# A graph kernel's prologue: the first block's rows gathered from x, row buffers placed lowest, fewer list loads

## The chip, the core and the metric

The kernel runs on one core of a Trainium2 chip. A core has five engines with their own instruction queues: TensorE (PE, with weight loads shown as PEld), VectorE (DVE), ScalarE (ACT), GpSimd (POOL) and SyncE (SP), which here only issues DMAs. All work in SBUF (128 partitions); TensorE writes PSUM. Times are microseconds of device time for one execution, and the metric is the median over executions. In the profile L12 means line 12 of the kernel, and `a<-b` means that an instruction writes tile `a` from tile `b`.

## What is computed

Two graph layers over the same 200,000 edges (`src`, `dst`, sorted by `dst`) and 6,250 nodes of 128 features. Cut to what matters here:

```python
h = jnp.maximum(_layernorm(x), 0.0)
# layer 0: attention over the edges that end in a node, 8 heads of 16
z = (h @ W).reshape(N, 8, 16)
el, er = einsum("nhp,hp->nh", z, attn_l), einsum("nhp,hp->nh", z, attn_r)
e = leaky_relu(el[src] + er[dst], 0.2)
a = exp(e - segment_max(e, dst)[dst])
x = x + segment_sum(z[src] * a, dst) / segment_sum(a, dst) + bias
h = jnp.maximum(_layernorm(x), 0.0)
# layer 1: a tensor product per edge, with weights from a small network on edge_attr_8
s, v = h[:, :32] @ W_up_s, einsum("nui,uw->nwi", h[:, 32:], W_up_v)
w = silu(silu(edge_attr_8 @ A1 + b1) @ A2 + b2) @ A3
x = x + segment_sum(products(s[src], v[src], edge_attr_4, w), dst) @ W_out
```

`z[src]` and `s[src], v[src]` are the costly part for data movement: each of the 200,000 edges takes one row of a table of nodes.

## The kernel before

Edges come in tiles of 128 (`P`), one edge to a partition, 1,563 of them (`TU`), and 16 tiles (`KB`) make a block, 98 blocks (`NB`) in each layer. Because the edges are sorted and the degrees even, the edges of a block end in few nodes, and a sum over edges is a matmul with a one-hot matrix. If the sorted ends are too uneven for that, a general kernel runs instead: a flag `ok_i` is computed first, all engines read it (`values_load`, L959) and branch (`tc.If`). Everything of the even case after the flag is in `even_edges`.

The prologue, in `tile_even_edges`, makes the table of layer 0. All of x (50 tiles of 128 nodes, in the order of a partition each, in chunks of 2, 3, 5, then 6 tiles, the last of 4) is loaded to `xs`. A loop over chunks runs as a software pipeline: mean and variance (`moments`), deviation, the normalised tile `fh` (shared out over ScalarE, VectorE and GpSimd by the tile's number), then groups of three tiles: transpose, relu to `h_t`, matmul with the extended weights `w_ext` (128 columns of z, 8 of el, 8 of er), copy to `zt`. z and el of a chunk go to the table `t0` in HBM (`to_table`, L792 to L798), er goes to `er_all` and is split into three bf16 parts in `er3`. Then GpSimd gathers the 16 row tiles of block 0 from `t0` into `z_first` (`gather`, L834: one indirect DMA for each tile of 128 edges, with the node numbers of `src_col`). The test for uneven edges compares each edge's end (`d_i`) with the one before it (`q_i`), two loads of the same list with a shift of one.

In `even_edges` SP first loads constants, then lists of ends, from which VectorE builds masks (`eq`, then `masks` on ScalarE), and the local ends `dloc`. A small transpose (`p_c`) gives `at`, the node numbers that SP uses to fetch single rows.

In the main loop the row tiles of a block lie in a buffer `g` of the pool `fz`, which has five (`z_pool`). GpSimd gathers them, up to three blocks ahead in the program; a buffer comes free when the sums of its block are done, a block later. In one block of three SP fetches the last tile by single rows (`rows_by_row`, L1078 to L1082, tile `r`), and in some blocks TensorE takes one tile out of a copy of the table in SBUF (`t0s`), which is loaded in the first four blocks (`split`, L1167).

Order. The order of TensorE, VectorE and ScalarE, in the main loops SP's too, is the order written (`tc.manual_schedule`). GpSimd and, in the prologue and the setup, SP are put in order by the framework from its own estimate. Each engine works its queue in order: what stands behind a waiting instruction waits too. Pools are laid out in SBUF in the order in which they are entered, and a tile that lies where an earlier pool's tile lay waits until that one's last reader and writer are done.

The pools at the head of `even_edges` are entered in this order:

```python
const = ctx.enter_context(tc.tile_pool(name="fconst", bufs=1))
z_pool = ctx.enter_context(tc.tile_pool(name="fz", bufs=5))
```

So the constants lie lowest, where the prologue's `fx` pool (`xs`, lists, weights) was.

Of the kernel before, what the change touches and what calls it, by code (L numbers as in the profile page):

```python
# [9 lines left out]
F32 = mybir.dt.float32  # L10
BF = mybir.dt.bfloat16
# [7 lines left out]
P = 128  # L19
# [722 lines left out]
def tile_even_edges(  # L742
# [46 lines left out]
    def to_table(table, of, i, n, eng):  # L789

        if i == 0:
            eng.dma_start(table[: P - W0, :], of[W0:, 0, :])  # L792
            if n > 1:
                to = table[P - W0 : n * P - W0]
                eng.dma_start(to.rearrange("(j p) f -> p j f", p=P), of[:, 1:n, :])
            return
        to = table[i * P - W0 : (i + n) * P - W0]
        eng.dma_start(to.rearrange("(j p) f -> p j f", p=P), of[:, :n, :])  # L798
# [20 lines left out]
    def deviation(pool, mv, n, name, m=P):  # L819
        rs = pool.tile([P, n, 1], F32, name=f"rs{name}")  # L820
        nc.scalar.activation(rs[:m], mv[:m, :, 1:2], AF.Sqrt, bias=eps[:m])
        return rs

    def normal(pool, mv, rs, n, name, m=P):

        nc.vector.reciprocal(rs[:m], rs[:m])
        mr = pool.tile([P, n, 1], F32, name=f"mr{name}")
        nc.vector.scalar_tensor_tensor(mr[:m], mv[:m, :, 0:1], -1.0, rs[:m], op0=OP.mult, op1=OP.mult)
        return rs, mr

    def gather(to, table, tiles, width, first=0):
        for t in tiles:
            k = first + t - tiles[0]
            nc.gpsimd.indirect_dma_start(  # L834
                out=to[:, k, :width], out_offset=None, in_=table,
                in_offset=bass.IndirectOffsetOnAxis(ap=src_col[:, t : t + 1], axis=0))
        return to

    def tiles_of(a, first):
        return a[first : first + TG * P * P].rearrange("(g t e) -> t g e", t=P, e=P)  # L840


    with tc.manual_schedule(engines={mybir.EngineType.PE, mybir.EngineType.DVE,
                                     mybir.EngineType.Activation}), \
# [11 lines left out]
        nc.scalar.sqrt(root, eps)  # L856
        w_ext = fx.tile([P, CW], F32, name="fw_ext")
# [9 lines left out]
        nc.sync.dma_start(src_col, srcc)  # L867
        d_i = fx.tile([P, TG, P], I32, name="fd_i")
        nc.sync.dma_start(d_i, tiles_of(dstt, P))
        q_i = fx.tile([P, TG, P], I32, name="fq_i")  # L870
        nc.sync.dma_start(q_i, tiles_of(dstt, P - 1))
        off = fx.tile([P, TG], F32, name="foff")
        nc.sync.dma_start(off, nums[:, NB * KB : NB * KB + TG])
# [7 lines left out]
        er_all = fx.tile([P, NX, H], F32, name="fer_all")  # L881
        NC = len(gx)
        mvs, rss, mrs, hs = {}, {}, {}, {}
        todo, done, outs = [], [], []
        for k in range(NC + 3):
            if 0 <= k - 1 < NC:
                rss[k - 1] = deviation(fp, mvs[k - 1], gx[k - 1][1], f"x{gx[k - 1][0]}")
            c = k - 2
            if 0 <= c < NC:
                i, n = gx[c]  # L890
                rs, mr = rss[c], mrs[c] = normal(fp, mvs[c], rss[c], n, f"x{i}")
                h = hs[c] = fp.tile([P, 10, P], F32, name="fh")
                for j in range(n):
                    by = (i + j) % 7
                    if by in ((2, 6) if c < NC - 2 else (2,)):
                        nc.scalar.activation(h[:, j, :], xs[c][:, j, :], AF.Identity,
                                             bias=mr[:, j, :], scale=rs[:, j, :])
                    else:
                        eng = nc.gpsimd if by in (0, 3, 5) and c < NC - 2 else nc.vector
                        eng.tensor_scalar(h[:, j, :], xs[c][:, j, :], mvs[c][:, j, 0:1],  # L900
                                          rs[:, j, :], op0=OP.subtract, op1=OP.mult)
            if k >= 3:
                i, n = gx[k - 3]
                zt = fp.tile([P, 10, CW], F32, name="zt")
                todo += [(k - 3, zt, j0, min(3, n - j0)) for j0 in range(0, n, 3)]
            while todo:
                c, zt, j0, m = todo.pop(0)
                p_t = fp_ps.tile([P, 4, P], F32, name="p_t")
                for j in range(m):
                    nc.tensor.transpose(p_t[:, j, :], hs[c][:, j0 + j, :], ident)  # L910
                h_t = fp.tile([P, 3, P], F32, name="h_t")
                nc.scalar.activation(h_t[:, :m], p_t[:, :m], AF.Relu)
                done.append((c, zt, j0, m, h_t))
                while len(done) > (1 if k < NC + 2 or todo else 0):
                    c, zt, j0, m, h_t = done.pop(0)
                    p_z = fp_ps.tile([P, 3, CW], F32, name="p_z")
                    for j in range(m):
                        nc.tensor.matmul(p_z[:, j, :], h_t[:, j, :], w_ext, start=True, stop=True)
                    outs.append((c, zt, j0, m, p_z))
                    while len(outs) > (1 if k < NC + 2 or todo or done else 0):  # L920
                        c, zt, j0, m, p_z = outs.pop(0)
                        copy = nc.scalar.copy if c < NC - 2 else nc.vector.tensor_copy
                        copy(zt[:, j0 : j0 + m, :], p_z[:, :m])
                        i, n = gx[c]
                        if j0 + m == n:
                            to_table(t0, zt[:, :, :ZW], i, n, nc.sync)
                            nc.gpsimd.tensor_copy(er_all[:, i : i + n, :], zt[:, :n, ZW:])
            if k < NC:
                i, n = gx[k]
                mvs[k] = moments(fp, xs[k], n, f"x{i}")  # L930
        gather(z_first, t0, range(KB), ZW)

        bad = fx.tile([P, TG, P], F32, name="fbad")
        nc.vector.tensor_tensor(bad, d_i, q_i, OP.is_lt)
        vs = fx.tile([P, 4], F32, name="fvs")
        nc.vector.tensor_reduce(vs[:, 0:1], bad.rearrange("p g e -> p (g e)"), AX.X, OP.add)
        w3 = fx.tile([P, 3, TG], F32, name="fw3")
        ef = fx.tile([P, 2, TG], F32, name="fef")
        nc.vector.tensor_sub(ef[:, 0, :], d_i[:, :, 0], off)
        nc.vector.tensor_sub(ef[:, 1, :], d_i[:, :, P - 1], off)  # L940
        nc.vector.tensor_single_scalar(w3[:, 0, :], ef[:, 0, :], 0.0, op=OP.is_lt)
        nc.vector.tensor_single_scalar(w3[:, 1, :], ef[:, 1, :], float(P), op=OP.is_ge)
        nc.vector.tensor_tensor(w3[:, 2, :], ef[:, 0, :], ef[:, 1, :], OP.is_equal)
        nc.vector.tensor_reduce(vs[:, 1:2], w3.rearrange("p a g -> p (a g)"), AX.X, OP.add)
        ones = fx.tile([P, 1], F32, name="fones")
        nc.vector.memset(ones, 1.0)
        p_v = fp_ps.tile([P, 4, P], F32, name="p_t")
        nc.tensor.matmul(p_v[:1, 0, :2], ones, vs[:, :2], start=True, stop=True)
        vr = fx.tile([1, 1], F32, name="fvr")
        nc.vector.tensor_reduce(vr, p_v[:1, 0, :2], AX.X, OP.add)  # L950
        nc.vector.tensor_copy(ok_i, vr)
# [14 lines left out]
def even_edges(tc, v):  # L966
# [5 lines left out]
    xp, dstc, y4, f8, bias, out, moments, deviation, normal, gather, tiles_of = (v[k] for k in (  # L972
        "xp", "dstc", "y4", "f8", "bias", "out", "moments", "deviation", "normal", "gather", "tiles_of"))
    with ExitStack() as ctx:
        const = ctx.enter_context(tc.tile_pool(name="fconst", bufs=1))
        z_pool = ctx.enter_context(tc.tile_pool(name="fz", bufs=5))
# [25 lines left out]
        wup = const.tile([P, P], F32, name="fwup")  # L1002
        nc.sync.dma_start(wup, v["wup"])
        a1p = const.tile([P, KB // 2, P], F32, name="fa1p")
        nc.sync.dma_start(a1p, v["a1p"])
        a2p = const.tile([P, P], F32, name="fa2p")
        nc.sync.dma_start(a2p, v["a2p"])
        b1 = const.tile([P, 1], F32, name="fb1")
        nc.sync.dma_start(b1, v["b1"])
        b2 = const.tile([P, 1], F32, name="fb2")  # L1010
        nc.sync.dma_start(b2, v["b2"])
# [9 lines left out]
        with tc.tile_pool(name="fbuild", bufs=1) as build:  # L1021
            d_c = build.tile([P, TU], I32, name="fd_c")
            nc.sync.dma_start(d_c, dstc)
            d_i = build.tile([P, TG, P], I32, name="fd_i")
            nc.sync.dma_start(d_i, tiles_of(dstt, P))
            q_i = build.tile([P, TG, P], I32, name="fq_i")
            nc.sync.dma_start(q_i, tiles_of(dstt, P - 1))
# [25 lines left out]
            nc.sync.dma_start(t1z[LATE * P - W0 :].rearrange("(j p) f -> p j f", p=P), zeros)  # L1053

# [933 lines left out]
```

## Time and profile before

| | us |
|---|---|
| median of 3 executions (3948.89 to 3955.46) | 3953.19 |
| profiled execution, its own time | 6235.86 |
| its span in the profile | 6234.0 |
| busy in the span: PE | 3133.4 |
| busy: POOL | 2872.4 |
| busy: DVE | 2620.8 |
| busy: ACT | 1190.7 |
| mean granted TensorE clock, of full speed | 0.728 |

How to read it: the profiled execution is much longer than the others, so what an instruction takes and the order in which things happen can be used, while the length of a wait cannot be carried over as it stands. A group's row gives its busy time, the mean of one instruction in ns, the engine's idle time just before those instructions, and what ended it. In the order of time a line gives the start, the time, engine, line, operation, tiles and a count. SPq is SP's DMA queue, and its time is that of issuing, not of moving the data.

### The profile page before, as it was taken

The numbers are of one execution on the slowest core, as the hardware profiler recorded it, in microseconds if no ns is written. First come the engines' busy times: TensorE is split into PE (matmuls) and PEld (weight loads), VectorE is DVE, ScalarE is ACT, GpSimd is POOL, SyncE is SP. The second block draws the span as 40 slices with busy tenths as digits, with TensorE's granted clock in tenths as the row PEclk, the third lists the DMA queues.
The fourth block names the chain that finished last, engine by engine and source line by source line (L and its number), as shares of the span: only waits on it lengthen the run. The fifth ranks groups of instructions, "written<-read, shape, count | busy, mean of one in ns | idle before, by whom it ended". The sixth has DMA issues, their size and how long they took to land. (4 is left out here: it accounts for less than half of the span.)

```text
span 6234.0 us, 64789 instructions
## 1 busy us (share of the span) xinstructions
PE 3133.4 (50%) x15554; PEld 2416.2 (39%) x15554; DVE 2620.8 (42%) x6094; ACT 1190.7 (19%) x3272; POOL 2872.4 (46%) x3052
## 2 busy tenths in 40 slices
PE   2145454444444444444355555555555555555557
PEld 1133333333333333333344444444444444444445
DVE  3244444444444444444333444444443444443446
ACT  1111111111111111111122222222222222222223
POOL 6144444444454454455534444444444444444442
PEclk6567677667667766777577777777777777777778
DMA  5122222222222222222111111111111111111111
GB/s 141 41 61 58 63 59 60 61 58 58 62 60 58 58 63 59 57 61 66 54 26 39 38 39 37 39 39 39 39 36 38 39 40 39 37 37 37 40 39 26
DMA packets 230951, 311.54 MB, mean 50 GB/s; under 512 B 83328, under 2 KB 168928, under 8 KB 230560
## 3 DMA queue, kind: packets, MB, share of 16 engines
q0 software_dynamic: 96640, 204.21, 13.8%
q1 hardware_dynamic: 133632, 103.03, 5.6%
q8 instruction: 125, 2.05, 0.1%
q14 instruction: 266, 2.18, 0.1%
q10 hardware_dynamic: 288, 0.07, 0.0%
HBM read 289.79 MB, written 16.95 MB: 49 GB/s over the span
## 5 line engine op out<-in xcount | busy, mean ns | idle before, releaser
L834 POOL DMA_INDIRECT g<-ft,fsrc x2980 | 2816.1, 945 | 3241.3 <-issue 1119.4
L1704 PE MATMUL p_u<-mj,s 128*128 128x256 f32 x3126 | 930.0, 450 | 680.8 <-DVE mj L1696 572.6
L1704 PEld LDWEIGHTS p_u<-mj,s 128*128 128x128 f32 x3126 | 682.6, 226 | 865.7 <-DVE mj L1696 623.4
L1251 DVE TENSOR_TENSOR d<-er_d,p_i 128x512 bf16<-128x512 bf16 x391 | 264.5, 677 | 863.1 <-DMA er_d<-fends_d 787.6
L1101 DVE TENSOR_TENSOR s<-p_i,fdloc 128x512 f32<-128x512 f32 x782 | 533.0, 682 | 197.2 <-PE p_i L1187 135.6
L1689 DVE TENSOR_TENSOR p_w<-g,p_w 128x128 f32<-128x128 f32 x387 | 112.9, 292 | 1178.2 <-ACT p_w L1671 1024.2
L1211 PE MATMUL p_x<-t0s,fz_first 128*128 128x408 bf16 (+1 forms) x2244 | 559.6, 409 | 29.9 <-issue 29.6
L1333 PE MATMUL p_u<-g,s 128*128 128x136 f32 x3062 | 537.4, 348 | 7.2 <-issue 4.4
L1671 ACT ACTIVATE p_w<-p_w,yb 128x64 f32<-128x64 f32 x1563 | 449.7, 288 | 461.2 <-remote 238.0
L1333 PEld LDWEIGHTS p_u<-g,s 128*128 128x128 f32 x3062 | 514.8, 255 | 7.7 <-issue 7.5
L1302 PE MATMUL pe<-mx,fshift 128*128 128x1 f32 (+1 forms) x194 | 55.8, 357 | 741.9 <-issue 514.7
L1667 PE MATMUL p_w<-fa3p,h 128*128 128x256 f32 x1564 | 422.7, 395 | 0.0
L1667 PEld LDWEIGHTS p_w<-fa3p,h 128*128 128x128 f32 x1564 | 303.3, 204 | 143.5 <-issue 106.0
L1657 ACT ACTIVATE h<-p_h,fb 128x512 f32<-128x512 f32 x196 | 134.7, 687 | 1141.9 <-remote 796.3
L1211 PEld LDWEIGHTS <-fz_first 128*128 128x128 bf16 x2244 | 250.8, 115 | 244.8 <-issue 152.5
L1719 PE MATMUL p_n<-fwout,m_t 128*128 128x128 f32 x192 | 57.6, 454 | 563.6 <-ACT m_t L1717 563.6
L1302 PEld LDWEIGHTS pe<-mx,fshift 128*128 128x128 f32 (+1 forms) x194 | 47.6, 305 | 749.9 <-issue 520.1
L1654 PE MATMUL p_h<-h,fa2p 128*128 128x512 f32 x392 | 248.0, 720 | 168.5 <-ACT h L1652 145.5
L1261 PEld LDWEIGHTS <-d 128*128 128x128 bf16 x1563 | 105.9, 122 | 513.0 <-DVE d L1251 378.0
L1687 DVE TENSOR_TENSOR vy<-g,p_i 128x384 f32<-128x384 f32 x387 | 211.3, 546 | 179.6 <-ACT p_i L1646 178.1
L1652 ACT ACTIVATE h<-p_h,fb 128x512 f32<-128x512 f32 x196 | 134.3, 685 | 726.8 <-PE p_h L1650 373.8
L1719 PEld LDWEIGHTS p_n<-fwout,m_t 128*128 128x128 f32 x192 | 43.7, 316 | 576.6 <-ACT m_t L1717 576.6
(220 smaller groups left out, 3667.6 us busy)
## 6 DMA issues: line engine op xcount, KB each, us to landing
r<-ft SPq DMA_DIRECT2D x3968, 0.5 KB
r<-ft SPq DMA_DIRECT2D x3968, 0.5 KB
er_d<-fends_d SPq DMA_DIRECT2D x98, 512.0 KB
g<-ft,fsrc POOLq DMA_INDIRECT x2980
ft<-in_e_f_dram SPq DMA_DIRECT2D x98, 64.0 KB
zr<-ft SPq DMA_DIRECT2D x24, 136.0 KB
yb<-in_e_y_dram SPq DMA_DIRECT2D x98, 32.0 KB
x<-in_e_xp_dram SPq DMA_DIRECT2D x48, 64.0 KB
```

The source lines that it names most:

```text
L834: nc.gpsimd.indirect_dma_start(out=to[:, k, :width], out_offset=None, in_=table, in_offset=bass.IndirectOffsetOnAxis(ap=src_col[:, t : t + ...
L1101: nc.vector.tensor_tensor(s[:, :m], iota[:, None, :].to_broadcast([P, m, P]), dloc[:, t : t + m].unsqueeze(2).to_broadcast([P, m, P]), OP. ...
L1211: nc.tensor.matmul(c["p_x"][:, :m, :], c["oh", k // half][:, k % half, :], t0s[:, s, i::NR, :], start=k == 0 and s == 0, stop=k == NR - 1 ...
L1251: nc.vector.tensor_tensor(d[:, :m], ends_row.tiles[c["b"]][:, k0 : k0 + m], node_p.unsqueeze(2).to_broadcast([P, m, P]), OP.is_equal)
L1333: nc.tensor.matmul(c["p_u"][:, :ZW], c["s"][k // 4][:, k % 4, :], c["z"][:, k, :], start=c["o"] + k == 0, stop=c["o"] + k == KT[c["b"]] - 1)
L1652: nc.scalar.activation(c["h1"], p_h, AF.Silu, bias=b1)
L1654: nc.tensor.matmul(p_h.rearrange("p q e -> p (q e)"), a2p, c["h1"].rearrange("p q e -> p (q e)"), start=True, stop=True)
L1657: nc.scalar.activation(h2, p_h, AF.Silu, bias=b2)
L1667: nc.tensor.matmul(w[:, k : k + n].rearrange("p k a u -> p (k a u)"), c["h2"][q // 4][:, q % 4, :], a3p[:, :n].rearrange("p k f -> p (k f) ...
L1671: nc.scalar.activation(w[:, k, ::2, :], w[:, k, ::2, :], AF.Copy, scale=c["yb"][:, k0 + k, 0:1])
L1687: nc.vector.tensor_mul(vy, v_n, y_p)
L1704: nc.tensor.matmul(blk[b]["p_u"][:, :MW], u["s"][:, k, :], u["mj"][:, k, :], start=k0 + k == 0, stop=k0 + k == KT[b] - 1)
```

## The change

Five things are done.

1. At the head of the prologue ScalarE loads the first 16 columns of the list of sources, and GpSimd gathers rows of x (not of `t0`) for block 0, straight into `z_first`. The loop over chunks becomes a function `rows_of`, which runs a second time over `z_first`, in three chunks of 6, 6 and 4 tiles, edge by edge, and writes z and el back into `z_first`.
2. GpSimd keeps only five of the `fh` tiles of the first pass, in chunks 6 and 7. VectorE takes the others, and the copies to `er_all`. `fh` and `zt` hold 6 tiles, and there are four `zt`.
3. The two shifted loads of the list of ends become one, 129 wide (`with_before`), in the prologue and in the setup. In the prologue the list loads stand after the table writes of chunks 1 and 3. The test counts through bf16 matmuls with ones, and stands ahead of the second pass.
4. The pool of the row buffers is entered ahead of the constants.
5. Five constants (`wup`, `a1p`, `a2p`, `b1`, `b2`) are loaded after the lists.

GpSimd and SP are put under the written order in the prologue as well.

```diff
+    def with_before(a):
+        t = tiles_of(a, P - 1)
+        return bass.AP(tensor=t.tensor, offset=t.offset,
+                       ap=[list(p) for p in t.ap[:-1]] + [[1, P + 1]])
     with tc.manual_schedule(engines={mybir.EngineType.PE, mybir.EngineType.DVE,
-                                     mybir.EngineType.Activation}), \
+                                     mybir.EngineType.Activation, mybir.EngineType.Pool,
+                                     mybir.EngineType.SP}), \
...
+        src_0 = fx.tile([P, KB], I32, name="fsrc0")
+        nc.scalar.dma_start(src_0, srcc[:, :KB])
         w_ext = fx.tile([P, CW], F32, name="fw_ext")
...
-        nc.sync.dma_start(src_col, srcc)
-        d_i = fx.tile([P, TG, P], I32, name="fd_i")
-        nc.sync.dma_start(d_i, tiles_of(dstt, P))
-        q_i = fx.tile([P, TG, P], I32, name="fq_i")
-        nc.sync.dma_start(q_i, tiles_of(dstt, P - 1))
+        d_i = fx.tile([P, TG, P + 1], I32, name="fd_i")
...
+        def load(k):
+            if k == 1:
+                nc.sync.dma_start(off, nums[:, NB * KB : NB * KB + TG])
+                nc.sync.dma_start(d_i, with_before(dstt))
+            elif k == 3:
+                nc.sync.dma_start(src_col, srcc)
...
+        row_0 = fx.tile([P, KB], I32, name="frow0")
+        nc.vector.tensor_single_scalar(row_0, src_0, W0, op=OP.add)
+        for k in range(KB):
+            nc.gpsimd.indirect_dma_start(
+                out=z_first[:, k, :P], out_offset=None, in_=xp,
+                in_offset=bass.IndirectOffsetOnAxis(ap=row_0[:, k : k + 1], axis=0))
...
+        def uneven_edges():
+            nc.vector.tensor_tensor(bad, d_i[:, :, 1:], d_i[:, :, :P], OP.is_lt)
...
+        def count_uneven():
...
+                nc.tensor.matmul(p_v[:1, :n], ones, b[:, k : k + n], start=k == 0, stop=False)
...
+        def rows_of(gx, xs, raw):
...
-                        eng = nc.gpsimd if by in (0, 3, 5) and c < NC - 2 else nc.vector
+                            late = by in (0, 3, 5) and NC - 4 <= c < NC - 2 and not raw
+                            eng = nc.gpsimd if late else nc.vector
...
+                if k == NC + 1 and not raw:
+                    uneven_edges()
+                for i, n, zt in ers:
+                    nc.vector.tensor_copy(er_all[:, i : i + n, :], zt[:, :n, ZW:])
...
+                    zt = z_first[:, i : i + n, :] if raw else fp.tile([P, 6, CW], F32, name="zt", bufs=4)
...
-                            nc.gpsimd.tensor_copy(er_all[:, i : i + n, :], zt[:, :n, ZW:])
...
-        gather(z_first, t0, range(KB), ZW)
...
+        rows_of(gx, xs, "")
+        count_uneven()
+        gz = [(k, min(6, KB - k)) for k in range(0, KB, 6)]
+        rows_of(gz, [z_first[:, k : k + n, :P] for k, n in gz], "e")
...
+        z_pool = ctx.enter_context(tc.tile_pool(name="fz", bufs=5))
         const = ctx.enter_context(tc.tile_pool(name="fconst", bufs=1))
-        z_pool = ctx.enter_context(tc.tile_pool(name="fz", bufs=5))
...
-            nc.sync.dma_start(d_i, tiles_of(dstt, P))
-            nc.sync.dma_start(q_i, tiles_of(dstt, P - 1))
+            d_q = build.tile([P, TG, P + 1], I32, name="fd_q")
+            d_i, q_i = d_q[:, :, 1:], d_q[:, :, :P]
+            nc.sync.dma_start(d_q, with_before(dstt))
```

## The prediction

> **What bounds the kernel now.** I read the page's engine rows first, then the order of time at the start, then the waits of the first 300 us.
>
> ```profile
> span 6234.0 us, 64789 instructions
> PE 3133.4 (50%) x15554; PEld 2416.2 (39%) x15554; DVE 2620.8 (42%) x6094; ACT 1190.7 (19%) x3272; POOL 2872.4 (46%) x3052
> L834 POOL DMA_INDIRECT g<-ft,fsrc x2980 | 2816.1, 945 | 3241.3 <-issue 1119.4
> ```
>
> The profiled execution took 6235.86 us: its span and 1.86 us around it. That is 1.58 times the median of 3953.19, so its stalls don't carry over, only durations and order. GpSimd (POOL) issues every gathered edge tile. Starts are 1.25 us apart when nothing holds them (59.33, 60.58, 61.84 in order of time: 0.94 busy, 0.30 gap), and the code has 3,021 gathers: 3,021 x 1.25 = 3,776 us, 96% of the median. So in unprofiled runs POOL's stream can hardly stand still: 177 us are left for what precedes it (42.5), for the last blocks' arithmetic and for all its stalls. What decides is when the stream starts and what stops it early.
>
> ```profile
> 38.65 1.88 DVE L934 TENSOR_TENSOR fbad<-fd_i,fq_i 128x1664 f32<-128x1664 int32 x1
> 42.51 1.17 POOL L834 DMA_INDIRECT fz_first<-ft,fsrc  x1 [1.91 <-issue]
> 45.76 0.37 DVE L958 CAST fer<-frest 128x400 bf16<-128x400 f32 x1
> 46.29 0.35 SPq L995 DMA_DIRECT2D fiota<-in_e_nums_dram  x1
> ...
> 53.91 0.45 SPq L1025 DMA_DIRECT2D fd_i<-in_e_dstt_dram  x1
> 55.04 1.73 SPq L1027 DMA_DIRECT2D fq_i<-in_e_dstt_dram  x1
> 56.81 5.53 SPq L1029 DMA_DIRECT2D fnxt<-in_e_dstt_dram  x1
> 63.08 0.94 POOL L834 DMA_INDIRECT g<-ft,fsrc  x1 [0.30 <-issue]
> 66.86 1.89 DVE L1041 TENSOR_TENSOR feq<-fd_i,fq_i 128x1664 f32<-128x1664 int32 x1 [17.39 <-issue]
> 76.18 5.49 ACT L1049 ACTIVATE fmasks<-feq 128x385 bf16<-128x385 f32 x13 [38.78 <-DVE feq L1046]
> 91.01 56.70 SPq L1082 DMA_DIRECT2D r<-ft  x22
> ```
>
> Two things run side by side after 39 us. POOL gathers block 0 (42.5 to 63.1), then blocks 1 to 5. The setup chain goes: SP's loads from 46.29, the lists landed at 66.86, 9.0 us of VectorE (to 75.87), masks on ScalarE (to 81.67), and SP's row by row loads from 91.01.
>
> ```profile
> POOL g L834 <- PE p_u L1333: 126.9, 1, 126.9
> 222.30 8.60 SPq L1082 DMA_DIRECT2D r<-ft  x20
> ```
>
> The first line, from the waits, is the important one. After 79 gathers POOL stands until block 1's row buffer is released, at the end of the third block. Undisturbed runs have a shorter wait of the same kind: before the first block may finish, SP must issue 152 single rows at 8.60/20 = 0.43 us, 65 us, from 91 to 156, and only then the table loads that close the block. Two more blocks follow before the buffer is free (over 195 us), while POOL wants it at 164. Here the setup chain, not POOL's start, sets when the stream goes on.
>
> **The change part by part**
>
> POOL. Removed: 16 gathers between 42.5 and 63.1 (16 x 1.25 = 20 us), 12 of 17 `fh` tiles and ten `fer_all` copies. Added: 16 gathers of x rows. They wait for a 16-column list, issued first on ScalarE's queue (0.4 us ahead of w0, which took from 0.90 to 3.58): start about 3.9, end 3.9 + 16 x 1.25 = 23.9 if nothing holds them. Queued behind them are the five `fh` tiles left to POOL (chunks 6 and 7). Block 0's rows were needed only at 121.9, when its logits are formed, so they stay hidden by the setup chain either way, with 60 us to spare.
>
> First pass. VectorE gets the tiles and copies. Per chunk of six: moments 1.73 (10.06 to 11.79), reciprocal and mean 0.36, four or five tiles at 0.27 (the run of five took 1.37), copies 0.1 to 0.2: 3.3 instead of 2.5. Adding the chunks with these terms, VectorE passes chunk 6's tiles at 24.5 and has its last moments at 28.6. Before it had got as far as chunk 8's moments by 21.4, but then lost time:
>
> ```profile
> 23.48 0.52 ACT L923 COPY zt<-p_z 128x432 f32<-128x432 f32 x1 [4.16 <-DMA ft<-zt]
> 28.13 0.85 PE L910 MATMUL p_t<-fident,fh 128*128 128x128 f32 x3
> 31.29 0.49 PE L910 MATMUL p_t<-fident,fh 128*128 128x128 f32 x3
> 23.40:30.00 6.60, 5.56 (x24) 5.54 (x25) 3.70 (x19) 5.45 (x14) 2.10 (x4) 0.50 0.45 133
> ```
>
> Table writes stood behind the list loads on SP, so `zt` was not free. The last row is a window, its last columns granted TensorE clock, DMA share and GB/s. The wait goes: those loads come after the third table write, and there are four `zt`. From 26.4 eight groups of three tiles remain at 1.07 us each (31.29, 32.35 and so on), so TensorE is through with them at 35.0, and with 2 us to the last copy (36.75 to 38.73 before) pass one ends near 37 instead of 38.7. The uneven test loses a 1.89 us reduction, gains bf16 matmuls (about 1 us) and its flag is there at 38 instead of 43.7. That alone buys nothing: see the waits.
>
> Second pass. 16 tiles, all new. VectorE from 38: moments of 12 tiles 3.5, then 0.36 + 5 x 0.27 + moments of four 1.2 = 2.9, then 1.7 and 1.45: tiles done at 47.5, the first ready for TensorE at 42.5. Six groups at 1.07 would end near 49; copy 50.3. Then the five `fer` steps (43.67 to 46.13, 2.5): E = 52.8. [...] TensorE idles about 4 us before pass two. The last rows show what followed 4 us of idleness before: granted clock 0.50 for 6.6 us, and groups 2.1 us apart (26.05, 28.13) instead of 1.07. [...] I take 56.
>
> The added waits. The new waits of the first gather of block 1 and of SP's first constant load reach past the flag: the gather waits for the last `fer` step, since its buffer now lies where the first pass's tiles were; `fiota` waits for the last matmul of pass two (E - 3), and everything on SP stands behind it. So POOL's stream for blocks 1 onward starts at E + 0.2 = 56.2 instead of 63.08: 6.9 earlier, not 20.
>
> SP's loads. They start at 53 instead of 46.3. Five constants are moved behind the lists (5 x 0.47 = 2.4); they then stand before the `fends` store, where SP waited 6.9 us for VectorE, so they cost nothing; without that wait, 2.4. `fer3o` waits for E. Then two of it, `fd_c`: the list goes out at E + 1.9 = 57.9. Before, `fd_i` went at 53.91 and the pair landed 13 us later. One list of 1664 runs holds the queue some 4 us (the two and the next took 53.9 to 62.3), so the joined load lands at about +8.5, 66.4, against 66.86. The 9 us of VectorE and all behind it follow: 0.5 earlier.
>
> Sum. The setup chain: 0.5 us earlier (E + 19.4 = 75.4 against 75.87), bounded by E = 52.8 (-3.7) and E = 62 (+5.5). POOL's start: -6.9, bounded by -10 and 0. As a buffer stops POOL at 164 us in the profile, and by the estimate above in unprofiled runs too, the chain's -0.5 is what reaches the end: 3953 - 0.5, with part of POOL's lead kept perhaps: 3952.
>
> Gathers beside VectorE. In the trace of before gathers take 1.50 instead of 0.94 beside the 1664-wide comparisons (68 to 76 us), and 0.94 beside the 128-wide `fshift` operations (48.97, 88.23). [...] I take nothing, because the form is the nearest; the upper end is the third case.
>
> **The rivals**
>
> A, the chain decides (0.47): 3952, 3944 to 3960. For it: the 126.9 us wait.
>
> B, POOL decides (0.30): if undisturbed rows of SP are much cheaper than 0.43 us, the third block ends before POOL needs its buffer, and the stream's earlier start comes through whole: -6.9 to -10, so 3943 to 3946. For it: the 96%. Against: the same wait.
>
> C, slower than before (0.20): the gathers of x rows run beside a VectorE that is always busy. At 1.50 + 0.30 each they end at 3.9 + 28.8 = 32.7, and the first of POOL's `fh` tiles is ready at 33.5 where TensorE wants it at 26.4. ScalarE and TensorE take their work in order, so pass one, pass two and E move by up to 7: E = 62 to 63. The chain is then 5.5 to 6.6 late: 3959 to 3960. If in unprofiled runs the second list never held the queue, 4 more: 3964. It decides from E = 56.5 for the chain, and it is over 0.2% from E = 64.4, or 60.4 without the list's credit.
>
> D, it does not do what it says (0.03): x rows that compete with the x loads (the windows give a DMA share of 1.1 to 1.2 from 6 to 23 us) hold the first pass itself; up to +10, 3963.
>
> **How the numbers follow.** About 0.2%, 7.9 us, is what a measurement of this kernel can tell from no change. Faster by more: 0.06 of A, 0.18 of B: 0.24. Slower: 0.07 of A (E late for another reason), 0.11 of C, 0.02 of D: 0.20. Between: 0.56. The time is A's, 3952. The range reaches from B's far end with some extra (3939) to C's (3964).
>
> **What would show it.** In the profile after: x-row gathers from about 4 us, 1.25 us apart (C: 1.8); the 4 us idle of ScalarE at `zt` gone; the flag at 38; the last `fer` step near 56; the first `g` gather just behind it; the joined list's comparison near 66; SP's rows near 91; and still a long wait of POOL for a matmul of the third block. I am wrong if that wait is not what limits unprofiled runs (then B), if rows start over 5 us later than 91 (C), or if the last `fer` step is before 50 us, where both gains would exceed 7 us.

## The result: no measurable difference

The changed kernel takes 3952.56 us (median of 12 executions, 3945.18 to 3954.54), the kernel before 3952.31 (median of 12, 3948.89 to 3955.46). The ratio is 0.9998, with a 95% interval of 0.999 to 1.0007.

Chips differ: on some this kernel takes 3950 to 3953 us, on others 6234 to 6296. The execution of before that is shown ahead of the prediction was of the second sort, that of after of the first. So before was profiled once more on a chip of the first sort (in the second set below), and all that follows compares runs of one sort.

The profiled execution of after took 3945.18 us, span 3943.1. From its page:

```profile
span 3943.1 us, 64944 instructions
PE 2776.7 (70%) x15605; PEld 2177.0 (55%) x15605; DVE 2639.6 (67%) x6171; ACT 1208.2 (31%) x3285; POOL 2860.9 (73%) x3030
L834 POOL DMA_INDIRECT g<-ft,fsrc x2980 | 2818.5, 946 | 1047.2 <-issue 884.9
```

GpSimd (POOL) is busy for 73% by the profile, but its gathers are 0.30 us apart even when nothing holds them, and 2,796 such gaps make most of the idle time. The waits of the whole run of after (us in total, times, longest):

```profile
POOL g L834 <- issue: 887.4, 2796, 3.8
POOL g L834 <- PE p_u L1379: 86.5, 62, 56.6
```

The order of time of after, the start:

```profile
3.67 1.09 POOL L900 DMA_INDIRECT fz_first<-in_e_xp_dram,frow  x1 [2.60 <-DVE stx L814]
5.07 0.96 POOL L900 DMA_INDIRECT fz_first<-in_e_xp_dram,frow  x1 [0.30 <-issue]
...
22.56 0.94 POOL L900 DMA_INDIRECT fz_first<-in_e_xp_dram,frow  x1 [0.30 <-issue]
23.95 4.21 POOL L952 TENSOR_SCALAR fh<-fxs,mvx,rsx 128x128 f32<-128x128 f32 x5 [0.44 <-PE p_t L967]
36.96 0.14 DVE L929 CAST fok<-fvr 1x1 int32<-1x1 f32 x1
40.95 1.58 PE L967 MATMUL p_t<-fident,fh 128*128 128x128 f32 x6 [4.74 <-DVE fh L952]
45.88 0.85 PE L967 MATMUL p_t<-fident,fh 128*128 128x128 f32 x3
47.77 0.49 PE L967 MATMUL p_t<-fident,fh 128*128 128x128 f32 x3
51.35 0.35 SPq L1041 DMA_DIRECT2D fiota<-in_e_nums_dram  x1
53.73 0.37 DVE L1003 CAST fer<-frest 128x400 bf16<-128x400 f32 x1
55.06 1.04 POOL L834 DMA_INDIRECT g<-ft,fsrc  x1 [26.90 <-DMA frsel<-in_e_rsel_dram]
55.99 0.44 SPq L1062 DMA_DIRECT2D fd_q<-in_e_dstt_dram  x1
64.69 1.89 DVE L1076 TENSOR_TENSOR feq<-fd_q 128x1664 f32<-128x1664 int32 x1 [9.35 <-DMA fd_q<-in_e_dstt_dram]
85.59 58.88 SPq L1128 DMA_DIRECT2D r<-ft  x152
144.99 8.61 SPq L1128 DMA_DIRECT2D r<-ft  x20
154.11 0.42 SPq L1218 DMA_DIRECT2D zr<-ft  x1
213.82 0.94 POOL L834 DMA_INDIRECT g<-ft,fsrc  x1 [56.57 <-PE p_u L1379]
```

Block 0's rows now come out of x while x is loaded. The second pass ends with the last `fer` step at 54.1, and GpSimd begins block 1 right behind it (the line of 55.06 names a load that landed about then, but in the trace GpSimd's queue moves on at 54.14, just behind that step's end at 54.10). Then come 79 gathers, and at 157 us GpSimd stands for 56.6 us, until TensorE has done block 1's sums.

The same places in the order of time of before, on a chip of the same sort:

```profile
62.57 0.94 POOL L834 DMA_INDIRECT g<-ft,fsrc  x1 [0.30 <-issue]
67.49 1.89 DVE L1041 TENSOR_TENSOR feq<-fd_i,fq_i 128x1664 f32<-128x1664 int32 x1 [18.59 <-DMA fq_i<-in_e_dstt_dram]
88.40 59.16 SPq L1082 DMA_DIRECT2D r<-ft  x152
157.20 0.42 SPq L1172 DMA_DIRECT2D zr<-ft  x1
216.81 0.94 POOL L834 DMA_INDIRECT g<-ft,fsrc  x1 [51.34 <-PE p_u L1333]
```

Set side by side (starts in us; the difference is after less before):

| | before | after | difference |
|---|---|---|---|
| first gather of block 1 | 62.57 | 55.06 | -7.5 |
| first comparison of the lists | 67.49 | 64.69 | -2.8 |
| first single row by SP | 88.40 | 85.59 | -2.8 |
| first table load for `t0s` | 157.20 | 154.11 | -3.1 |
| GpSimd begins to stand (start of the next gather less its wait) | 165.5 | 157.3 | -8.2 |
| block 1's buffer is free | 216.81 | 213.82 | -3.0 |
| last gather | 3932.3 | 3926.3 | -6.0 |

This table is the result in small. GpSimd's lead of 7.5 to 8.2 us is there until it stands, and what comes out of the stand is the lead of the setup chain, 3.0. The last gathers lie 6.0 apart, but after was profiled in the fastest of its 12 executions, 7.4 us under their median, and before in one at the median of its set, and the 12 executions of each kernel spread over 6.6 (before) and 9.4 us (after), so nothing can be read from the last row. Three us are 0.08% of the time, inside the interval of the medians.

### The profile page after: what moved, and what is told of

The parts are those of the page before. It is cut to its first block, busy times and chain, and to the rows that moved or that the text cites. A ratio compares the mean times of both kernels' runs of the same rounds, so it can differ in the third digit from the quotient of the medians.

```text
span 3943.1 us, 64944 instructions
## 1 busy us (share of the span) xinstructions
PE 2776.7 (70%) x15605; PEld 2177.0 (55%) x15605; DVE 2639.6 (67%) x6171; ACT 1208.2 (31%) x3285; POOL 2860.9 (73%) x3030
## 5 line engine op out<-in xcount | busy, mean ns | idle before, releaser
L1750 PE MATMUL p_u<-mj,s 128*128 128x256 f32 x3126 | 785.3, 395 | 178.7 <-DVE mj L1742 177.3
L1750 PEld LDWEIGHTS p_u<-mj,s 128*128 128x128 f32 x3126 | 588.2, 195 | 340.4 <-DVE mj L1742 264.3
L1379 PE MATMUL p_u<-g,s 128*128 128x136 f32 x3062 | 491.1, 329 | 0.4 <-DVE g L1374 0.4
L1257 PE MATMUL p_x<-t0s,fz_first 128*128 128x408 bf16 (+1 forms) x2244 | 473.9, 365 | 0.0
L1379 PEld LDWEIGHTS p_u<-g,s 128*128 128x128 f32 x3062 | 469.0, 235 | 0.5 <-DVE g L1374 0.4
L1257 PEld LDWEIGHTS <-fz_first 128*128 128x128 bf16 x2244 | 229.6, 105 | 160.1 <-issue 33.3
L1696 PE MATMUL p_h<-ft,fa1p 128*128 128x128 f32 x1568 | 222.8, 288 | 94.2 <-DMA ft<-in_e_f_dram 94.2
L1696 PEld LDWEIGHTS p_h<-ft,fa1p 128*128 128x128 f32 x1568 | 213.5, 201 | 118.7 <-issue 100.3
L1374 DVE TENSOR_TENSOR g<-g,pe 128x1024 f32<-128x1024 f32 x193 | 234.6, 1216 | 5.0 <-ACT g L1365 4.7
L1737 DVE TENSOR_REDUCE vd<-vy 128x128 f32<-128x384 f32 x391 | 229.8, 588 | 0.0
```

Source lines behind the costliest of these rows:

```text
L1257: nc.tensor.matmul(c["p_x"][:, :m, :], c["oh", k // half][:, k % half, :], t0s[:, s, i::NR, :], start=k == 0 and s == 0, stop=k == NR - 1 ...
L1374: nc.vector.tensor_mul(zh, zh, p_a[:, k0 : k0 + m].unsqueeze(3).to_broadcast([P, m, H, D]))
L1379: nc.tensor.matmul(c["p_u"][:, :ZW], c["s"][k // 4][:, k % 4, :], c["z"][:, k, :], start=c["o"] + k == 0, stop=c["o"] + k == KT[c["b"]] - 1)
L1696: nc.tensor.matmul(p_h[:, q, :], a1p[:, q0 + q, :], c["ft"], start=True, stop=True)
L1737: nc.vector.tensor_reduce(vd, vy.rearrange("p t i u -> p t u i"), AX.X, OP.add)
L1750: nc.tensor.matmul(blk[b]["p_u"][:, :MW], u["s"][:, k, :], u["mj"][:, k, :], start=k0 + k == 0, stop=k0 + k == KT[b] - 1)
```

## The experiments

The ratios are to runs of the kernel before on the same chip in the same set. Two theories run through them. A: the setup chain, through SP's rows and table loads, decides when block 1's buffer comes free, and GpSimd's earlier start is lost while it stands. B: GpSimd's start decides.

**First set, on a chip where before takes 6236.4 us (29 executions).**

The kernel before, once more:

> The kernel before, unchanged, for an undisturbed trace to set beside that of after. Theory A (the setup chain on SP decides): SP's single rows begin within 1 us of the 85.6 of after, and GpSimd stands some 50 us before block 1's buffer is free, at 213 to 215 us as in after. Theory B (GpSimd's start decides): the gathers of block 1 start 7 us later than in after and the buffer's release too comes 7 us later. Theory D (the chain came 5 us earlier and it was lost later in the kernel): rows begin near 91 and the release comes near 219, and the 5 us are given back after the first blocks.

6246.18 us, like the profile shown ahead of the prediction: rows begin at 91.02, and the buffer is free at 290.6. It ran on a chip of the second sort, and so says nothing of the traces above.

GpSimd held up by 20 us:

```diff
                                            and not (c["b"] in dense and k % KB == KD)], ZW)
+                    if g == 1:
+                        gather(c["z"], t0, range(t, t + c["kt"]), ZW)
```

> After, with GpSimd held up on purpose: each of block 1's 16 gathers is issued twice into the same buffer, 16 x 1.25 = 20 us more for GpSimd and nothing for any other engine. Theory A (GpSimd's lead is swallowed while it stands for block 1's buffer): its standing shrinks from 56.6 to some 35 us and the time stays within 2 us of after's 3952.6. Theory B (GpSimd's start decides): +20, 3973.

6265.70 us, ratio 1.0043 (1.0031 to 1.0055). On this sort of chip the time does rise, by some 27 us over before by the ratio, as theory B has it.

SP's setup held up by repeating its first load:

```diff
-        nc.sync.dma_start(iota, nums[:, NB * KB + TG : NB * KB + TG + P])
+        for _ in range(10):
+            nc.sync.dma_start(iota, nums[:, NB * KB + TG : NB * KB + TG + P])
```

> After, with SP's setup held up on purpose: its first constant load is repeated ten times into the same tile, each waiting for the one before, some 20 us (9 x 2 to 2.5). Theory A: single rows begin near 105 instead of 85.6, the release of block 1's buffer moves from 213.8 to about 233, and the time goes up by as much as SP was held up: 3970 to 3974. Theory B: the time stays at 3952 to 3954.

6233.68 us, ratio 0.9993 (0.9983 to 1.0003). The experiment missed its aim: the framework put the other setup loads between the repeats (the first eight went out 1.9 to 4.7 us apart), and SP's first loads of `er_d` began at 93.73, while they begin at 92.60 in after on a chip of this sort. It says nothing of either theory.

Rows of layer 0 one block ahead instead of three:

```diff
-                rows_until(rows, g + 0.5)
+                rows_until(rows, g - 1.5)
...
-                rows_until(rows, g + 1)
+                rows_until(rows, g - 1)
```

> After, with SP's single rows in layer 0 fetched one block ahead instead of three: 86 rows instead of 158 stand on SP ahead of the first table loads. Theory A: 72 x 0.386 = 28 us less before these loads (154 to 126), buffer free near 186 instead of 213.8, GpSimd's first long standing near 29 instead of 56.6, and the time falls by about as much, 3924 to 3930, unless rows come late for their blocks afterwards. Theory B: GpSimd loses nothing there that counts, 3952.

6213.90 us, ratio 0.9965 (0.9953 to 0.9978). The buffer is free at 256.7 instead of before's 290.6, 34 us earlier, and the median falls by 22 us. That is theory A's direction, if not its size.

**Second set, on a chip where before takes 3949.57 us (9 executions).**

The kernel before, once more:

> The kernel before, unchanged, once more: the first look fell on a chip on which all executions take about 6236 us. Where the time is near 3952: theory A (the setup chain decides): SP's single rows begin within 1 us of the 85.6 of after and block 1's buffer is free within 2 us of after's 213.8. Theory D (the chain came earlier and the lead was lost later): rows begin near 91, the release comes near 219, and the difference is given back behind it.

3949.23 us, with the trace set beside after's above. The rows begin 2.8 us later than in after and the release comes 3.0 later: more than A's 1 and 2, but the same shift in both, which is A's claim. B's 7 for the release does not show, and neither do D's 5. This is one trace of each kernel.

Table loads ahead of the rows, in after and in before:

```diff
-                rows_until(rows, g + 0.5)
...
-                rows_until(rows, g + 1)
+                lead = -1 if g == 1 else min(1, max(0, (g - 3) / 4))
+                if g:
+                    rows_until(rows, g + 1 - 3 + lead)
```

> After, with SP's order in the first blocks of layer 0 changed: the first block's table loads stand ahead of the single rows, and rows are fetched at most one block ahead. First table load near 88 instead of 154, the second block's near 118 instead of 184, block 1's buffer free near 148. Theory A (rows ahead of the table loads hold GpSimd): its standing of 56.6 us goes to under 5 and the time falls by 50 to 68, to 3885 to 3902. Rival (rows fetched late hold later blocks, or the start doesn't count): 3940 or more. On a chip where single rows take longer while gathers run, the gain is larger, 70 or more.

> The same edit of SP's order in the kernel before. Theory A with the lead swallowed: without the standing GpSimd's start decides, and this kernel should be later than after with the same edit by the 7 us by which its first gather of block 1 is later (63.1 against 55.1), or by up to 8. Rival (the lead is worth nothing for another reason, such as slower gathers): the two are within 2 us.

After with this edit takes 3971.90 us, ratio 1.0054 (1.004 to 1.0067); before with it 3970.71, ratio 1.0054 (1.004 to 1.0068). Both are slower by 21 us, where theory A expected 50 to 68 less; the time is on the rival's side (3940 or more). The first table load did move from 154.11 to 89.82, as the order of time of after with this edit shows, and GpSimd no longer stood before block 1's buffer: its longest stand was 27.6 us, before block 2's, not 56.6:

```profile
89.82 0.43 SPq L1218 DMA_DIRECT2D zr<-ft  x1
205.52 0.94 POOL L834 DMA_INDIRECT g<-ft,fsrc  x1 [27.55 <-PE p_u L1379]
```

What was won was given back block by block. The starts of SP's loads of `er_d`, one a block, give the period of layer 0 over 60 blocks, from the 21st to the 81st: (1706.7 - 544.8) / 60 = 19.37 us in before, (1700.7 - 538.6) / 60 = 19.37 in after, and (1717.2 - 524.1) / 60 = 19.88 in after with the table loads first. Counted with those of block 0, the 200th gather is 24.5 us earlier than in after, the 800th 0.9 later, the 1,400th 25.2 later. The waits of this kernel show GpSimd's gaps grown from 887.4 to 940.5:

```profile
POOL g L834 <- issue: 940.5, 2800, 5.0
POOL g L834 <- PE p_u L1379: 43.7, 54, 27.6
```

Why the period grew no run settles, since the edit did two things: it shortened SP's lead from three blocks to one at most, and it took away the call that put rows ahead of the node stores (`ft<-sv`) in each block, so that all of them stand behind the stores. The rival's reason, rows that come late, does not show in the trace: ScalarE's copy of a fetched tile (L1142, 31 in layer 0) never waited for its rows, the last of which was issued at least 7.5 us before it. What it shows is SP standing at the stores until ScalarE has made `sv`. The waits of SP's queue from 600 to 1800 us, in after:

```profile
SPq L1128 <- DMA er_d<-fends_d: 50.8, 42, 1.7
SPq L1448 <- DVE g L1265: 4.1, 12, 0.6
```

and in after with the table loads first:

```profile
SPq L1446 <- ACT sv L1437: 41.6, 20, 3.3
SPq L1128 <- DMA er_d<-fends_d: 29.0, 29, 1.4
```

All waits together, SP's queue waits 84 us there and 61 in after. That is 23 us more in 1,200, where the longer period costs about 31 (estimate: 1200 x 0.51 / 19.88). So the place of the rows in each block, not their lead, is the likelier cause. A run with the rows left ahead of the stores would tell.

The pair speaks against GpSimd's start once more. In before with the edit the first gather of block 1 is at 63.5, in after with it at 55.6. The stands end 3.1 us apart, as the order of time of before with the edit shows beside the line above, and the medians, on one chip, differ by 1.2 us, the wrong way for B and within the rival's 2. But GpSimd still stood in both, so what its start is worth without any stand was not tested:

```profile
208.60 0.94 POOL L834 DMA_INDIRECT g<-ft,fsrc  x1 [21.82 <-PE p_u L1333]
```

**Third set, on a chip where before takes 6296.29 us (27 executions).**

After, unchanged:

> After, unchanged, timed on the same chip as the kernel before. The two undisturbed traces put after's single rows 2.8 us earlier (85.59 against 88.40), its first table load 3.1 us earlier (154.11 against 157.20) and its last gather 6.0 us earlier (3926.3 against 3932.3), although medians were equal. Theory S (in layer 0 SP's stream of single rows sets the pace, so its start counts): 2 to 4 us faster than before. Rival B (GpSimd's start, 7.5 us earlier, counts): 6 to 8 faster. Rival N (what is won at the start is lost in the main loops): within 1.

6291.33 us, ratio 0.9992 (0.9984 to 1.0): 5 us less, not to be told from nothing, so it decides between none of the three.

GpSimd held up by the same 20 us, once more:

> After, with each of block 1's 16 gathers issued twice into the same buffer: 20 us more for GpSimd and nothing for another engine. On a chip that runs the kernel before in about 3950 us: theory S (SP's stream counts in layer 0 and GpSimd has to wait for it anyway): GpSimd's standing of 56.6 us shrinks to about 36, time within 2 us of after. Rival B: +20. On a chip where it takes 6236 us: +20 or more, as before.

6331.77 us, ratio 1.0055 (1.0041 to 1.0068): 40 us over after. Block 1's buffer is free at 312.0 instead of 294.3. The two profiled executions differ by 19 us (6309.28 against 6290.21), about what the release moved; the median of five executions (6309 to 6341) lies 22 us above the profiled one, and no trace shows that part.

The list of ends loaded three times:

```diff
-            nc.sync.dma_start(d_q, with_before(dstt))
+            for _ in range(3):
+                nc.sync.dma_start(d_q, with_before(dstt))
```

> After, with the joined list of ends loaded three times into the same tile, one after the other: the setup chain is later by two such loads (8.7 us each from issue to landing), and nothing else changes. On a chip that runs the kernel before in about 3950 us: theory S: single rows begin 17 to 20 us later and the time rises by as much, 3966 to 3970. Rival B (GpSimd's start counts): no more than 2 us.

6298.53 us, ratio 1.0001 (0.9992 to 1.0011). The loads overlapped in part: the chain was later by 9.8 us (first `er_d` at 102.44 against 92.60). The buffer was free at 295.1 against 294.3, and the median is 7 us over after's, with intervals that overlap. So on this sort of chip 20 us on GpSimd move the release by 17.7, and 10 us on the setup chain move it by 0.8: here B is right. A trait of such chips that fits this is told at the end. On a chip of the first sort neither delay was run.

Fewer single rows in layer 0:

```diff
+        by_0 = [b for b in range(4, NB - 2) if b % 4 == 0]
...
-            for b in by_row:
+            for b in (by_0, by_row)[layer]:
...
-        def rows_until(rows, block):
+        def rows_until(rows, block, every=3):
...
-            while rows_until.n < (block + 3) * P / 12 and next(rows, 0) is None:
+            while rows_until.n < (block + 3) * P / 4 / every and next(rows, 0) is None:
...
-                                           if not (c["b"] in by_row and k % KB == KB - 1)
+                                           if not (c["b"] in by_0 and k % KB == KB - 1)
...
-                rows_until(rows, g + 0.5)
+                rows_until(rows, g + 0.5, 4)
...
-                rows_until(rows, g + 1)
+                rows_until(rows, g + 1, 4)
```

> After, with SP fetching one tile by single rows in every fourth block of layer 0 instead of every third (24 tiles instead of 32; GpSimd gathers the 8 others; layer 1 unchanged). SP's rows per block fall from 42.7 to 32, GpSimd gets 8 x 1.25 = 10 us more. Theory S: block period of layer 0 (19.37 us between loads of `er_d` in both undisturbed traces) falls to GpSimd's own need, 15.3 x 1.25 = 19.1, which gives 96 x 0.27 = 26 us, and 44 rows less stand ahead of the first table loads, 17 us: 3907 to 3925. Rival P (GpSimd sets the pace of layer 0): period up by 0.1, time 10 us up less what the start gives, 3945 to 3962. Rival L (another engine's loop sets it): period the same.

6274.19 us, ratio 0.9958 (0.9945 to 0.9972). By the count of rows it is 23 tiles instead of 31, not 24 instead of 32. The buffer is free at 270.2, 24 us earlier than in after. The period of layer 0 is 29.86 against 29.69. It did not fall, and the rise is no larger than the difference between traces of kernels with after's main loop on such chips (29.46 to 29.74). Yet SP now stands 330 us at the node stores between 600 and 1800 us, where it stood less than 1 in after. So SP's rows are not what sets the period here. GpSimd's own need (theory P, up by 0.1) is not either: it starts a gather in 1.95 us there, not 1.25. That leaves theory L, and what was won came from the start.

**Fourth set, on a chip where before takes 6234.64 us (11 executions).** Fewer rows as in the third set, and the table loads ahead of them:

```diff
-                rows_until(rows, g + 0.5, 4)
...
-                rows_until(rows, g + 1, 4)
+                lead = -1 if g == 1 else min(3, (g - 3) / 4)
+                if g:
+                    rows_until(rows, g + 1 - 3 + lead, 4)
```

> After, with two edits of SP's single rows in layer 0: every fourth block instead of every third, and the first block's table loads ahead of the rows (none of them in block 0, 32 in block 1, then caught up by a quarter of a block in each block, to three blocks ahead). On a chip that runs the kernel before in about 3950 us: theory S (SP's stream sets the pace of layer 0): block 1's buffer free near 160 instead of 213.8, as in the run with the table loads first, and now the gain isn't given back: period of layer 0 19.1 instead of 19.37; together 24 + 26 us less, 3900 to 3910. Rival L (another engine's loop sets the pace): period 19.4 or more, 3928 or later. On a chip where it takes 6240 to 6300, whose single rows take 2.5 us beside gathers: the 128 rows ahead of the table loads go, some 60 us, and the period stays near 29.8: 1% faster.

6183.47 us, ratio 0.9918 (0.9899 to 0.9936), 51 us less. The buffer is free at 218.2 us, the period is 29.83: about the 1% that was expected. This version beats before on this sort of chip by 0.8%; after, which the third set could not tell from before, was not run beside it. On the other sort it was not run, and the pair of the second set warns that this order of SP can cost more there than it brings.

## Why the prediction was right, and where it was not

The forecast was 3952, by the case in which the setup chain decides; 3952.56 came. Its steps:

- *x-row gathers from 3.9, 1.25 apart, end 23.9.* They ran from 3.67 to 23.5, the first in 1.09, the others in 0.94 to 0.96 each, beside a VectorE that was busy for 3.93 to 3.96 of every 4 us from 8 to 24. VectorE's `fh` tiles didn't lengthen them: five from 14.52 took 1.37 us, beside gathers of 0.94 and 0.95. So the `fshift` row was the right one to go by. The third case is refuted for this sort of chip.
- *Flag at 38, first transpose of pass two at 42.5, E at 56.* Flag 37.1, transpose 40.95, E = 54.1. TensorE did idle for 4.74 us before pass two, and its granted clock was 0.51 from 40.9 to 47.7 us and 1.00 from 47.7 to 51: six transposes took 1.58 us and the next three 0.85, from 47.77 on three took 0.49. So the step on the clock held, at 6.8 us of half clock where the row of before had 6.6. From first transpose to E, 13.15 us were measured; by the row it was 13.5 (42.5 to 56, with three groups later by 1.05 us each), and 10.3 without a penalty. The row, which I took, comes nearer. E came 1.9 us early mainly because pass two began 1.55 us early: the flag by 0.9, and VectorE's first tiles by 0.65 more.
- *First `g` gather behind the last `fer` step, 6.9 earlier.* 55.06, 7.5 earlier than before.
- *The list issued at 57.9, landed at 66.4; the chain 0.5 earlier.* Issued 55.99, compared at 64.69: 8.7 from issue to comparison, 8.5 predicted. The chain is 2.8 earlier than in before on the same sort of chip. This is the mis-sized term: 1.9 of the missing 2.3 us are E, through the early start of pass two. It also stood against a trace of the other sort of chip, whose comparison began at 66.86, not 67.49.
- *SP needs 65 us for the rows ahead of the table loads.* 172 rows, 20 more than I counted, in 68.0 us (85.59 to 153.60). That is 0.40 us a row, 0.39 for the first 152, not 0.43. Two errors partly cancelled.
- *A buffer stops GpSimd, in unprofiled runs too; free over 195, wanted at 164.* Free at 213.8, wanted at 157.3. This was the step on which all hung, and it held: the lead on GpSimd of 7.5 to 8.2 became the chain's 3.0.
- *"In unprofiled runs POOL's stream can hardly stand still", from 3,776 us of gathers in 3953.* This step failed as a bound for layer 0. The traces have 2,996 gathers (2,980 of `g` and 16 for block 0), so it is 3,745 us and 95%. GpSimd stands 68 us in two waits before block 1's and block 2's buffers, and later in layer 0 for short whiles (2.6 us before the gather at 1026.06, for one). From 600 to 1800 us after starts 940 gathers, one in 1.28 us; from 3000 to 3400, in layer 1, 320, one in 1.25. So layer 0 has a pace of its own a little slower than GpSimd's, which gives GpSimd's lead no use there. Had the 96% been true of every stretch, case B would have been right. Which loop sets 19.37 stays open. SP's rows fill most of it (42.7 rows a block at 0.39 are 16.7 us, `er_d`, x and stores come on top), and by the waits shown above SP's queue waits mostly for its own loads. But on the other sort of chip its queue was as full in after (some 15 us of waits in the same stretch), and fewer rows did not shorten the period there; on this sort they were not tried.

So the time moved from one place to another and not away. Sixteen gathers left GpSimd's queue between 42 and 62; the second pass that they need took most of it back, since block 1's gathers wait for its end. Of the 7.5 us that were left, all but the chain's 3.0 were lost in the stand before block 1's buffer. That two kernels with different starts take the same time rests on this stand in the traces and on the pair of the second set; delays of GpSimd or of the chain alone ran only on the other sort of chip. And luck had a part in how close 3952 came: the chain's lead was taken as 0.5 us and was 2.8 to 3.0, and these 3 us are below what the runs can tell.

## What to carry to other kernels

Before moving work off an engine, find the next place where that engine stands and ask which chain ends that stand: only that chain's lead comes out on the other side. A share of the whole time says little; count the period of each stage, and compare it with the engine's own need in that stage. And an edit at the head of a queue that works in order can change every later block: the rows ahead of the table loads looked like the delay, but the edit that moved them also moved rows behind each block's stores, where SP then stood, and the time rose by 21 us.

## What was not expected of the hardware

In a stretch in which GpSimd issues gathers, the other engines started far fewer instructions on a chip of the second sort than on one of the first. The two lines are windows from 12 to 24 us of one kernel, after, first on a chip of 3950 us, then on one of 6296 (busy us and instructions of PE, PEld, DVE, ACT, POOL, then granted clock, DMA share, GB/s). First:

```profile
12.00:24.00 12.00, 10.02 (x59) 8.76 (x60) 11.86 (x76) 8.95 (x25) 8.81 (x11) 1.00 0.92 248
```

then:

```profile
12.00:24.00 12.00, 3.10 (x12) 2.22 (x11) 3.20 (x17) 1.55 (x4) 8.77 (x10) 1.00 0.46 125
```

GpSimd's gathers of x rows take the same time in both. The others start 12 instead of 59 matmuls and 17 instead of 76 instructions of VectorE, at full granted clock and with the DMAs half as busy. This speaks for the gathers, not the chip alone: before, which has none at that time, starts 51 matmuls and 62 instructions of VectorE in these 12 us on a chip of either sort. And it sets in late: from 4 to 12 us, beside the same gathers, VectorE starts 37 instructions against 42. In that second run the first pass stands until the gathers end, as its waits and its order of time show:

```profile
ACT rsx L821 <- remote: 11.2, 1, 11.2
```

```profile
35.95 4.21 POOL L952 TENSOR_SCALAR fh<-fxs,mvx,rsx 128x128 f32<-128x128 f32 x5 [12.44 <-PE p_t L967]
```

So here the x-row gathers seem to hold the first pass, by 12 us (ScalarE goes on at 26.4, 2.9 us after the last of them), though not by VectorE's doing as the third case had it. SP is hit too. The order of time of SP from 90 to 130 us, in after on the chip of 3950:

```profile
89.97 39.95 SPq L1128 DMA_DIRECT2D r<-ft  x102
```

and on the chip of 6296:

```profile
98.77 29.15 SPq L1128 DMA_DIRECT2D r<-ft  x14
```

That is 0.39 us a row against 2.1. Over 600 to 1800 us, the start of a row comes 0.83 us after that of the row before on the second chip if a gather runs in between, and 0.43 if none does; on the first it is 0.40 and 0.39. SP's register moves for the rows, too, took up to 0.71 us in the run with rows one block ahead, on a chip of the second sort (97 to 199 us, median 0.03), where they took 0.03 to 0.04 in after on the first. This fits the third set, where GpSimd's start moved the release of block 1's buffer and the setup chain hardly did: SP's rows go quickly only once the gathers of the first five blocks are through. Of the 172 rows ahead of the table loads, 29 are issued by the end of the 79th gather at 169.3 us, and the other 143 in the 65 us behind it. What in the chip makes it so, no run here shows.

A second, smaller thing: gathers beside VectorE's 1664-wide comparisons of integers took 1.39 to 2.25 us in after (65 to 74 us), instead of 0.94, and beside the 128-wide operations of the first pass 0.94 to 0.96.
